# A mixture-of-experts layer that starts on full tiles: the last block's output and routing as steps between the experts' products

## The chip, the cores and the metric

The kernel runs on one core of a Trainium2 chip. The metric is the device time of one execution in microseconds (us). The engines of a core are TensorE (PE; its weight loads are listed as PEld), VectorE (DVE), ScalarE (ACT), GpSimd (POOL) and SyncE (SP), which here only starts transfers and reads the registers that they need. A transfer is started ("issued") by an engine's queue and carried out by the core's 16 DMA engines.

## The reference

A picture of 64 x 64 points with 256 channels goes through four layers. Only the last two matter here. Written out for N = 4096 tokens t of C = 256 channels:

```python
# layer 3, attention: one head, all tokens
n = layernorm(t); q, k, v = n @ Wq + bq, n @ Wk + bk, n @ Wv + bv
t = t + softmax(q @ k.T / 16) @ v
# layer 3, mixture of 8 experts, the two best for each token
n = layernorm(t); probs = softmax(n @ Wg + bg); w, e = top_k(probs, 2); w = w / w.sum()
t = t + sum(w[r] * (gelu(n @ W1[e[r]] + b1[e[r]]) @ W2[e[r]] + b2[e[r]]) for r in (0, 1))
```

W1 is 256 x 1024 and W2 is 1024 x 256 for each expert. Layer 2 ends in a mixture of the same form with a hidden size of 256 and its own weights. Everything is float32.

## The kernel before

**Blocks and tiles.** The 4096 tokens are 8 blocks of 512 (`NBLK`, `NB`), each of 4 groups of 128 (`TPB`). Every token is listed at two experts, so 8192 rows stand in a list in DRAM (`xs`), one stretch of 4096 rows for each expert. The expert work goes in tiles of 256 rows of one expert (`MT`). An expert's last tile may be partly filled, so up to 39 tiles may be needed (`NTILE`); 36 of them (`MOST`) are always worked out, and the last three stand under a condition that the counts decide.

**Attention (`attn3`, L2385).** For each block of queries, 16 steps (`g`, with 16 pairs of key groups) run on PE: `scores(g)`, and two steps later (`LAG`) `values(g - 2)`. Both are products in a form with seven instead of eight block products, so DVE adds and subtracts parts before and after them (L2534 to L2537, L2552, L2570 to L2572), and ACT takes the exponentials (L2566). After the last step of a block its output stands in `oT`. `finish` (L2595) multiplies it by the value weights for one group of 128, divides, and adds to the tokens `t`. In the steps of the next block, indices j = 0 to 3 finish the four groups of the previous block, j = 4 starts its `route`, and j = 6, 8, 10, 12, 14 each run one of the routing's five stages:

1. statistics, square root (ACT), norm, all on DVE but the root
2. transposing one half of the channels on PE (`turn`, L2061), copied by ACT
3. transposing the other half, copied by DVE
4. the router's logits (16 small matmuls), the two best experts (`top2`, DVE), the exponential (ACT), weights, and the running count per expert (`cum`)
5. positions of the rows in the lists (a small product on PE, `place`), `find` on DVE, and 8 scatters of 128 rows each to `xs` by POOL (L2113)

In this part the order on PE and POOL is the one written (`tc.manual_schedule`), and the other engines are ordered by a planner. The last block, number 7, has no next block to be hidden under: its four `finish` and all five routing stages follow after attention's last matmul (L2662 to L2666), and then `tile_table` (L2121), about 40 small DVE instructions. The table says for each tile which expert it belongs to (`tab[:, 0]`), where its rows begin (`tab[:, 1]`), and how many are valid.

**Experts (`experts`, L2173; `expert_tiles`, L2190).** For each tile, SP reads expert and row from the table into registers and loads the tile's rows (260 KB) and the expert's weights w1 and w2 (1028 and 1152 KB; L2204, L2209, L2211), two tiles ahead. `turn` transposes the rows on PE, `first` makes the hidden rows with 32 matmuls and Gelu on ACT, `sides` makes four sums of weights on POOL (`f_wt`, L2259), `where` finds the target rows and weights on DVE, and `second` multiplies by w2, again with seven products, and scatters the result to DRAM (`ys`, L2302). The loop runs `first` of tile i, `turn` of tile i + 1, then `second` of tile i - 1. The planner orders all engines. The same code serves layer 2, with sizes of its own.

**Memory.** SBUF and PSUM are given out in pools that open and close with the stages. Attention's pools (`a3`, `a3w`, `a3_ps`) hold the values, the working tiles and the routing's `room` (the normed rows that the scatters read). They close before the expert pools (`f3e`, `f3e_ps`) open. PSUM has 8 banks; in the expert stage the transposed rows have two, the hidden rows three, the two parts of the output three.

Of the kernel before, what the change touches and what calls it, by code (L numbers as in the profile page):

```python
# [29 lines left out]
NE = 8  # L30
# [19 lines left out]
NI = MT // P  # L50

# [37 lines left out]
class Net:  # L89
# [2031 lines left out]
    def tile_table(self, S, wp, bank):  # L2121


        nc = self.nc
        tl = lambda shape, tag, dt=F32: wp.tile([P] + shape, dt, tag="f_" + tag, name="f_" + tag, bufs=1)
        c_ps = bank()[:, :NE]
        self.mm(c_ps, [(self.all_one, S["cum"])])

        ci = tl([NE], "ci", I32)
        nc.vector.tensor_copy(ci, c_ps)  # L2130
        nc.vector.tensor_single_scalar(ci, ci, MT - 1, ALU.add)
        nc.vector.tensor_single_scalar(ci, ci, MT.bit_length() - 1, ALU.arith_shift_right)
        cnt = tl([NE], "cnt")
        nc.vector.tensor_copy(cnt, ci)
        ends = tl([NE], "ends")
        nc.vector.tensor_tensor_scan(ends, self.one.to_broadcast([P, NE]), cnt, 0.0, ALU.mult, ALU.add)

        last = tl([1], "last")
        nc.vector.tensor_scalar_add(last, ends[:, NE - 1 : NE], -1.0)
        tau = tl([NTILE], "tau")  # L2140
        nc.vector.tensor_scalar(tau, self.count, last, None, ALU.min)
        past = tl([NTILE, NE], "past")
        nc.vector.tensor_tensor(past, bc(ends, 1, NTILE), bc(tau, 2, NE), ALU.is_le)
        ex = S["ex"]
        nc.vector.tensor_reduce(ex, past, AX.X, ALU.add)
        tab = S["tab"]
        nc.vector.tensor_scalar_mul(tab[:, 0, :], ex, float(P))
        nc.vector.tensor_tensor(past, past, bc(cnt, 1, NTILE), ALU.mult)
        skip = tl([NTILE], "skip")
        nc.vector.tensor_reduce(skip, past, AX.X, ALU.add)  # L2150
        nc.vector.tensor_sub(tau, tau, skip)
        nc.vector.tensor_scalar_mul(tau, tau, float(MT))
        nc.vector.scalar_tensor_tensor(skip, ex, float(N), tau, ALU.mult, ALU.add)
        nc.vector.tensor_copy(tab[:, 1, :], skip)
        rows = tl([NE], "rows")
        nc.vector.tensor_copy(rows, c_ps)
        nc.vector.tensor_copy(S["used"], ends[:, NE - 1 : NE])

        nc.vector.tensor_tensor(past, bc(ex, 2, NE), bc(self.count[:, :NE], 1, NTILE), ALU.is_equal)
        nc.vector.tensor_tensor(past, past, bc(rows, 1, NTILE), ALU.mult)  # L2160
        nc.vector.tensor_reduce(skip, past, AX.X, ALU.add)
        nc.vector.tensor_sub(skip, skip, tau)
        nc.vector.tensor_scalar(tau, self.count, last, None, ALU.is_le)
        nc.vector.tensor_mul(skip, skip, tau)

        nc.vector.tensor_tensor(S["in"], bc(self.nth[:, :NI], 1, NTILE), bc(skip, 2, NI), ALU.is_lt)
        nc.vector.tensor_scalar(S["off"], S["in"], -1.0, 1.0, ALU.mult, ALU.add)
        for i in range(0, NTILE, 4):
            n = min(4, NTILE - i)
            part = S["off"][:, i : i + n, :].rearrange("p i k -> p (i k)")  # L2170
            nc.vector.scalar_tensor_tensor(part, self.nth[:, : n * NI], float(2 * N), part, ALU.add, ALU.mult)

    def experts(self, S):  # L2173

        tc = self.tc

        def some(tiles):
            with (
                tc.tile_pool(name=f"f{S['L']}e", bufs=5 if S["L"] == 2 else 3) as wp,
                tc.tile_pool(name=f"f{S['L']}e_ps", bufs=1, space=PSUM) as ps,  # L2180
            ):
                self.expert_tiles(S, tiles, wp, ps)

        some(range(MOST))
        used = self.nc.values_load(S["used"][0:1, 0:1], min_val=0, max_val=NTILE,
                                   skip_runtime_bounds_check_because="worked out from counts of tokens")
        with tc.If(used > MOST):
            some(range(MOST, NTILE))

    def expert_tiles(self, S, tiles, wp, ps):  # L2190
        nc, A = self.nc, self.A
        L, tab = S["L"], S["tab"]
# [5 lines left out]
        def load(i):  # L2198
            e = nc.values_load(tab[0:1, 0, i : i + 1], engines=[mybir.EngineType.SP], min_val=0, max_val=(NE - 1) * P,
                               skip_runtime_bounds_check_because=why)  # L2200
            row = nc.values_load(tab[0:1, 1, i : i + 1], engines=[mybir.EngineType.SP], min_val=0, max_val=NE * N - MT,
                                 skip_runtime_bounds_check_because=why)
            x = wp.tile([P, NI, CX], F32, tag="x", name="f_x", bufs=ahead + 3)
            rows = lambda: nc.sync.dma_start(out=x, in_=self.xs[bass.ds(row, MT), :].rearrange("(i p) c -> p i c", p=P))  # L2204

            if i > 0:
                rows()
            w1 = wp.tile([P, 2 * hidden + KH], F32, tag="w1", name="f_w1")
            nc.sync.dma_start(out=w1, in_=A[f"f{L}_w1"][bass.ds(e, P), :])  # L2209
            w2 = wp.tile([P, KH * C + C], F32, tag="w2", name="f_w2")  # L2210
            nc.sync.dma_start(out=w2, in_=A[f"f{L}_w2"][bass.ds(e, P), :])  # L2211
            if i == 0:
                rows()
            return x, w1, w2

        def turn(x):
            p = ps.tile([P, 2, MT], F32, tag="x", name="f_x_ps", bufs=2)
# [17 lines left out]
        def where(i, x):  # L2235
# [3 lines left out]
            op = nc.vector  # L2239
            op.tensor_scalar(first, x[:, :, C + 3], S["ex"][:, i : i + 1], None, ALU.is_equal)  # L2240
# [4 lines left out]
            op.tensor_tensor(to, to, S["in"][:, i, :], ALU.mult)  # L2245
            op.tensor_tensor(at, to, S["off"][:, i, :], ALU.add)
# [60 lines left out]
        tiles = list(tiles)  # L2307

        nc.scalar.activation(wp.tile([P, 1], F32, tag="g", name="f_gelu", bufs=1), self.one, AF.Gelu)
        ld = {i: load(i) for i in tiles[:ahead]}  # L2310
        xT = turn(ld[tiles[0]][0])
        to = where(tiles[0], ld[tiles[0]][0])
        done = None
        for i in tiles:
# [4 lines left out]
            now = (i, h, w2, sides(w2)) + to  # L2319
            if i < tiles[-1]:  # L2320
                xT = turn(ld[i + 1][0])
                to = where(i + 1, ld[i + 1][0])
            if done is not None:
                second(*done)
            done = now
        second(*done)

    def outputs(self, b, y):

        src = self.ys[: 2 * N, :].rearrange("(r b p i) c -> b p r (i c)", r=2, b=NBLK, i=TPB)  # L2330
        for r in range(2):
            (self.nc.sync, self.nc.scalar)[r].dma_start(out=y[:, r].rearrange("p i c -> p (i c)"), in_=src[b][:, r])
# [10 lines left out]
    def moe_state(self, pool, L=2):  # L2343
        tl = lambda shape, tag, dt=F32: pool.tile([P] + shape, dt, tag=tag, name="f_" + tag)
        return {
            "L": L, "to": tl([2, NT], "to", I32), "tab": tl([2, NTILE], "tab", I32), "used": tl([1], "used", I32),
            "big": tl([2, 2, NT // 2], "big"), "r": tl([NT], "r"), "ex": tl([NTILE], "ex"), "in": tl([NTILE, NI], "in"), "off": tl([NTILE, NI], "off"),
# [37 lines left out]
    def attn3(self, t, S):  # L2385
# [6 lines left out]
        with (  # L2392
            tc.tile_pool(name="a3", bufs=1) as pool,
            tc.tile_pool(name="a3d", bufs=1, space=DRAM) as dpool,
        ):

# [8 lines left out]
            wvp = pool.tile([P, 2, C + 1], F32, tag="wvp", name="a3_wvp")  # L2405
# [12 lines left out]
            with (  # L2418
                tc.tile_pool(name="a3w", bufs=2) as wp,
                tc.tile_pool(name="a3_ps", bufs=1, space=PSUM) as ps,  # L2420
            ):
# [4 lines left out]
                def bank(few=False):  # L2426
                    banks.append(banks.pop(0))
                    return ps.tile([P, NB], F32, tag=banks[-1], name="a3_q_ps")

                room = lambda: wp.tile([P, TPB * CX + 2 * NB], F32, tag="room", name="f_room")  # L2430
# [3 lines left out]
                def add(b):  # L2434

                    y = room()[:, : 2 * TPB * C].rearrange("p (r i c) -> p r i c", r=2, c=C)
                    self.outputs(b, y)
                    part = t[:, b * TPB : (b + 1) * TPB, :]
                    for r in range(2):
                        nc.vector.tensor_tensor(part, part, y[:, r], ALU.add)  # L2440
# [33 lines left out]
                def ask(b, m):  # L2474

                    ks = kss[b]
                    if m == 0:
                        nc.vector.memset(vs[:, 2 * b : 2 * b + 2, 1 : 4 : 2, P - 1 : P], 1.0)

                        qTs[b] = wp.tile([P, 2, NB], F32, **(dict(tag="oT", name="a3_qT", bufs=1) if b else dict(tag="q", name="a3_q")))  # L2480
# [14 lines left out]
                def route(t0, T):  # L2495
                    r = room()
                    n = r[:, : TPB * CX].rearrange("p (i c) -> p i c", c=CX)
                    rT = r[:, TPB * CX :].rearrange("p (k n) -> p k n", k=2)
                    return self.route(t0, T, t, S, wp, n, rT, bank)
# [75 lines left out]
                def values(g):  # L2575
# [11 lines left out]
                    if j == NPAIR - 1:  # L2587
                        oT = oTs[b] = wp.tile([P, 2, 2, QB], F32, tag="oT", name="a3_oT", bufs=1)
# [55 lines left out]
                with tc.manual_schedule(engines={ET.PE, ET.Pool}):  # L2644
                    steps = iter(())
                    for g in range(first, G + LAG):
# [6 lines left out]
                        if b > 0:  # L2653
# [4 lines left out]
                            elif j % 2 == 0:  # L2658
                                next(steps, None)
                    for _ in steps:  # L2660
                        pass
                    banks += ["sa", "sb", "sc"]  # L2662
                    for i in range(TPB):
                        finish(NBLK - 1, i)
                    for _ in route((NBLK - 1) * TPB, TPB):
                        pass  # L2666
                with tc.manual_schedule(engines={ET.PE, ET.Pool, ET.DVE}):
                    self.tile_table(S, wp, bank)
# [88 lines left out]
    def run(self, x, out):  # L2757
        tc, nc = self.tc, self.nc
        with tc.tile_pool(name="const", bufs=1) as cpool, ExitStack() as left:
# [20 lines left out]
            with tc.tile_pool(name="tok", bufs=1) as tpool:  # L2780
# [5 lines left out]
                with tc.tile_pool(name="moe", bufs=1, side="right") as mpool:  # L2786
# [9 lines left out]
                    self.experts(S)  # L2796
# [127 lines left out]
```

## Time and profile before

| What | us |
|---|---|
| median of 10 runs | 3423.87 |
| fastest and slowest of them | 3421.54, 3433.22 |
| the profiled execution's own time | 3433.52 |
| its span, first to last instruction | 3431.8 |
| PE busy in the span | 3105.9 (91%) |
| DVE busy | 2303.8 (67%) |
| ACT busy | 1328.7 (39%) |
| POOL busy | 1455.5 (42%) |

The profile's page gives busy time by engine, then the span in 40 equal slices of 85.8 us, a digit for the busy tenths in each, then the granted TensorE clock (PEclk) in the same slices. A timeline row holds the start in us from the span's start, its length, engine and line, the operation with what it writes and reads, the shape, and how many instructions are put together; in brackets stands how long the engine had been idle before and what ended it. A q behind the engine's name marks an instruction of its queue. Layer 3's attention runs from about 1930 to 2835 us, its experts to about 3381 us.

### The profile page before, as it was taken

Reading aid. Unit: us, or ns where it says so; the run is one execution under the profiler, and the core shown is the slowest. Engines: PE = TensorE matmul, PEld = TensorE weight load, DVE = VectorE, ACT = ScalarE, POOL = GpSimd, SP = SyncE. Lnnn points to the kernel's source line nnn. Section 1 sums busy time; section 2 is a strip of 40 time slices with the busy share of each in tenths; the row PEclk is TensorE's granted clock in tenths of the full one; section 3 lists DMA queues with packets and bytes.
Section 4 is the critical chain, followed back from the end, with each engine's and each line's share of the span. In section 5 each row is a group of like instructions: output and inputs, shape, how many; then the busy total and the mean of one; then the engine's idle time right before and its main releaser. Section 6 shows DMA issues by size and latency. Waiting matters only on the chain.

```text
span 3431.8 us, 66162 instructions
## 1 busy us (share of the span) xinstructions
PE 3105.9 (91%) x25772; PEld 2324.7 (68%) x25772; DVE 2303.8 (67%) x5315; ACT 1328.7 (39%) x2550; POOL 1455.5 (42%) x1316
## 2 busy tenths in 40 slices
PE   6779999999977899897969789999999996999997
PEld 3443444344436888666847567888888885999996
DVE  8885777577754677796855576777777775555552
ACT  4444344444425666243633352222222222333331
POOL 2028788878834555343544352000000003555552
PEclk9889999999988999897979899999999997999998
DMA  1145555521133222100158643322333314555554
GB/s 71 43 113 145 160 154 169 133 65 52 49 122 106 68 75 74 42 1 2 64 198 266 208 182 107 104 87 93 99 99 99 98 56 160 194 196 208 205 199 175
DMA packets 241688, 407.01 MB, mean 119 GB/s; under 512 B 78353, under 2 KB 152850, under 8 KB 231890
## 3 DMA queue, kind: packets, MB, share of 16 engines
q1 hardware_dynamic: 212002, 344.40, 31.7%
q0 software_dynamic: 13056, 35.93, 2.8%
q10 hardware_dynamic: 16304, 22.31, 2.0%
q8 instruction: 207, 3.39, 0.4%
q14 instruction: 119, 0.97, 0.1%
HBM read 287.07 MB, written 111.30 MB: 116 GB/s over the span
## 4 chain that ended last, share of the span: by engine, by line
PE 42%; DVE 9%; DMA 6%; issue 5%; ACT 3%; POOL 3%; SPq 0%; POOLq 0%; DVEq 0%; ACTq 0%
PE a_sa_ps L2547 6%; PE f_h_ps L148 5%; DMA ys<-f_y,f_at 3%; PE l_acc_ps L1156 3%; PE a_oa_ps L2586 3%; PE a_ob_ps L2586 3%; PE a_oc_ps L2586 3%; PE a_sb_ps L2547 3%; PE f_ya_ps L148 2%; PE f_yb_ps L148 2%; DVE l_pr L1152 2%; PE a_od_ps L2586 1%; POOL ys L2302 1%; PE a_q_ps L148 1%; PE a_sc_ps L2547 1%
## 5 line engine op out<-in xcount | busy, mean ns | idle before, releaser
L772 ACT COPY l_sc<-l_s 128x384 f32<-128x384 f32 (+1 forms) x632 | 304.0, 532 | 451.2 <-PE l_s L765 440.6
L777 DVE TENSOR_TENSOR l_sm<-l_s,mask 128x256 f32<-128x256 f32 (+2 forms) x628 | 307.9, 550 | 90.5 <-PE l_s L765 89.4
L148 PE MATMUL f_h_ps<-f_xT,f_w 128*128 128x256 f32 x1440 | 340.7, 388 | 21.8 <-DVE f_xT L2222 13.1
L2113 POOL DMA_INDIRECT xs<-f_room,f_to x64 | 64.3, 1004 | 697.3 <-issue 582.6
L148 PEld LDWEIGHTS f_h_ps<-f_xT,f_w 128*128 128x128 f32 x1440 | 262.2, 192 | 85.5 <-ACT f_h L2232 29.6
L765 PE MATMUL l_s<-l_q,l_k 32*128 32x256 f32 (+3 forms) x2944 | 270.4, 453 | 0.0
L2566 ACT ACTIVATE a_e<-a_e 128x512 f32<-128x512 f32 x256 | 155.9, 629 | 246.0 <-DVE a_e L2536 242.9
L782 POOL TENSOR_TENSOR l_sm<-l_sc,mask 128x768 f32<-128x768 f32 (+1 forms) x116 | 202.4, 1752 | 87.8 <-ACT l_sc L772 87.7
L2232 ACT ACTIVATE f_h<-f_h_ps,f_w 128x256 f32<-128x256 f32 x360 | 166.6, 470 | 187.9 <-PE f_h_ps L148 187.9
L1152 DVE TENSOR_TENSOR l_pr<-l_vk,l_w_ps 128x1280 f32<-128x1280 f32 x128 | 186.7, 1481 | 55.2 <-PE l_acc_ps L1156 37.6
L765 PEld LDWEIGHTS l_s<-l_q,l_k 32*128 32x128 f32 x2944 | 132.3, 183 | 115.2 <-issue 67.5
L2302 POOL DMA_INDIRECT ys<-f_y,f_at x144 | 146.5, 1018 | 142.8 <-ACT f_y L2301 112.7
L1156 PE MATMUL l_acc_ps<-ident,l_pr 128*128 128x128 f32 x1600 | 198.2, 278 | 7.7 <-POOL l_pr L1147 7.6
L1156 PEld LDWEIGHTS l_acc_ps<-ident,l_pr 128*128 128x128 f32 x1600 | 184.8, 144 | 14.2 <-POOL l_pr L1147 8.6
L786 POOL TENSOR_TENSOR l_sm<-l_sc,mask 128x256 f32<-128x256 f32 (+1 forms) x220 | 184.9, 868 | 15.4 <-ACT l_sc L772 14.5
L2259 POOL TENSOR_TENSOR f_wt<-f_w 128x512 f32<-128x512 f32 x72 | 89.9, 1270 | 216.6 <-PE f_ya_ps L148 205.0
L2547 PE MATMUL a_sa_ps<-a_q,a_kt 128*128 128x256 f32 x512 | 155.3, 385 | 13.6 <-DVE a_u L2552 12.8
L2551 ACT COPY a_u<-a_sa_ps 128x256 f32<-128x256 f32 x128 | 47.6, 372 | 293.0 <-PE a_sa_ps L2547 293.0
L811 PE MATMUL l_b_ps<-l_sm,l_v 128*32 128x256 f32 (+2 forms) x2176 | 153.4, 372 | 0.0
L2547 PE MATMUL a_sa_ps<-a_qt,a_kt 128*128 128x256 f32 x512 | 152.4, 379 | 0.0
L782 POOL TENSOR_TENSOR l_sm<-l_sc,mask_c 128x768 f32<-128x768 f32 (+1 forms) x64 | 120.1, 1894 | 37.0 <-ACT l_sc L772 36.5
L2547 PE MATMUL a_sb_ps<-a_qt,a_kt 128*128 128x256 f32 x512 | 132.3, 381 | 0.0
(558 smaller groups left out, 7290.1 us busy)
## 6 DMA issues: line engine op xcount, KB each, us to landing
a_kt<-a_kd SPq DMA_DIRECT2D x128, 512.0 KB
f_w<-in_f_w SPq DMA_DIRECT2D x36, 1152.0 KB
f_w<-in_f_w SPq DMA_DIRECT2D x36, 1028.0 KB
xs<-zero SPq DMA_DIRECT2D x8, 4160.0 KB
l_vk<-vt SPq DMA_DIRECT2D x180, 128.0 KB
f_x<-xs SPq DMA_DIRECT2D x72, 260.0 KB
f_w<-in_f_w SPq DMA_DIRECT2D x36, 384.0 KB
l_rcp<-l_recd SPq DMA_DIRECT2D x48, 256.0 KB
```

Source lines behind the costliest of these rows:

```text
L148: self.nc.tensor.matmul(out, lhsT, rhs, start=(i == 0), stop=(i == len(pairs) - 1))
L765: nc.tensor.matmul(s[pair, j][:, at : at + m, :], key(hp), qs[hp], start=(z == 0), stop=(z == len(pieces) - 1))
L772: nc.scalar.copy(sc[:, j], s[1, j])
L777: nc.vector.tensor_tensor(to(pair, j, kind, at), pick(s[pair, j], kind, which), mask, ALU.mult)
L782: nc.gpsimd.tensor_tensor(out[:, :, at, :], of[:, :, which, :], bc(mask, 1, 2), ALU.mult)
L786: nc.gpsimd.tensor_tensor(to(1, j, kind, at), pick(sc[:, j], kind, which), mask, ALU.mult)
L1152: nc.vector.tensor_tensor(pr, vk, bc(held["w"][:, j, dy], 3, D), ALU.mult)
L1156: nc.tensor.matmul(acc[:, m, j, :], pf[:, dx, m * P : (m + 1) * P], self.ident, is_transpose=True, start=(j == 0 and dy == 0 and dx == 0 a ...
L2232: nc.scalar.activation(h[:, m, :], q, AF.Gelu, bias=w1[:, 2 * hidden + m : 2 * hidden + m + 1])
L2302: nc.gpsimd.indirect_dma_start(out=self.ys_parts[(i % 4) * NI + k], in_=y[:, k, :], in_offset=None, out_offset=bass.IndirectOffsetOnAxis(a ...
L2547: mm = lambda out, i, right: nc.tensor.matmul(out, A[i], right, start=True, stop=True)
L2586: nc.tensor.matmul(out, vs[:, j, i, :], right, start=(j == 0 and side != 1), stop=(j == NPAIR - 1 and side != 0))
```

## The change

- A new table, `full_table`, is made from the counts of blocks 0 to 6 alone. 7168 of the 8192 rows are known by then, and at most 255 of each expert's rows don't fill a tile, so at least 20 tiles (`FULL`) are full whatever block 7 adds. They are table "A". `gone` notes how many tiles of each expert it holds. `tile_table`, when called early, makes table "B" of the 19 others, from the counts of all blocks less `gone`; for layer 2 it makes all 39 as before.
- Block 6's routing stages run at j = 5 to 9, one at each step of the loop, and `full_table` at j = 10.
- Attention's pools close directly after the loop. What block 7 still needs stands in two pools opened before them, `k3` and `k3_ps`: the value weights, the output `oT`, the routing's `room` (one instead of two) and small tiles, and one PSUM bank.
- `experts` gets seven steps, run one at a time: the four `finish` before the first tile's rows are turned, then the first routing stage, then one stage after `first` of tile 0, after `first` of tile 1, after `second` of tile 0, and after `first` of tile 2; after `second` of tile 1 table B is made. Block 7's rows are thus scattered to `xs` when the rows of tiles 0 to 4 have been asked for, and before those of tile 5.
- PE's order in the third layer's experts is the one written, and the transposed rows have one PSUM bank there instead of two.
- `add`, which fetches layer 2's results at attention's start, takes three rooms for half a fetch each instead of two for a whole one.

The diff, cut to its core:

```diff
+FULL = (2 * (N - NB) - NE * (MT - 1)) // MT
+    def full_table(self, S, wp, bank):
+        T, n = S["A"], FULL
+        c_ps = bank()[:, :NE]
+        self.mm(c_ps, [(self.all_one, S["cum"])])
+        nc.vector.tensor_copy(ci, c_ps)
+        nc.vector.tensor_single_scalar(ci, ci, MT.bit_length() - 1, ALU.arith_shift_right)
+        nc.vector.tensor_copy(full, ci)
+        nc.vector.tensor_tensor_scan(ends, self.one.to_broadcast([P, NE]), full, 0.0, ALU.mult, ALU.add)
+        nc.vector.tensor_tensor(past, bc(ends, 1, n), bc(self.count[:, :n], 2, NE), ALU.is_le)
+        nc.vector.tensor_reduce(T["ex"], past, AX.X, ALU.add)
+        nc.vector.tensor_scalar_mul(T["tab"][:, 0, :], T["ex"], float(P))
+        nc.vector.tensor_tensor(past, past, bc(full, 1, n), ALU.mult)
+        nc.vector.tensor_reduce(tau, past, AX.X, ALU.add)
+        nc.vector.tensor_sub(tau, self.count[:, :n], tau)
+        nc.vector.tensor_scalar_mul(tau, tau, float(MT))
+        nc.vector.scalar_tensor_tensor(tau, T["ex"], float(N), tau, ALU.mult, ALU.add)
+        nc.vector.tensor_copy(T["tab"][:, 1, :], tau)
+        nc.vector.tensor_sub(gone, full, ends)
+        nc.vector.tensor_scalar(gone, gone, float(n), 0.0, ALU.add, ALU.max)
+        nc.vector.tensor_tensor(gone, gone, full, ALU.min)
+        nc.gpsimd.memset(T["in"], 1.0)
+        nc.gpsimd.memset(T["off"], 0.0)
...
+        if early:
+            nc.vector.tensor_sub(cnt, cnt, S["gone"])
...
-        some(range(MOST))
+        tiles = [("A", i) for i in range(FULL)] if early else []
+        rest = [("B", i) for i in range(NTILE - len(tiles))]
+        tiles += rest[:-3]
...
+                if early:
+                    order.enter_context(tc.manual_schedule(engines={mybir.EngineType.PE}))
+                self.expert_tiles(S, tiles, wp, ps, list(steps), 1 if early else 2)
...
-            p = ps.tile([P, 2, MT], F32, tag="x", name="f_x_ps", bufs=2)
+            p = ps.tile([P, 2, MT], F32, tag="x", name="f_x_ps", bufs=x_banks)
...
         ld = {i: load(i) for i in tiles[:ahead]}
+        step()
         xT = turn(ld[tiles[0]][0])
         to = where(tiles[0], ld[tiles[0]][0])
+        step()
         done = None
         for i in tiles:
...
             now = (i, h, w2, sides(w2)) + to
+            step()
             if i < tiles[-1]:
...
                 second(*done)
+                step()
...
-                    y = room()[:, : 2 * TPB * C].rearrange("p (r i c) -> p r i c", r=2, c=C)
-                    self.outputs(b, y)
+                    ys = [wp.tile([P, TPB, C], F32, tag="room", name="f_room", bufs=3) for r in range(2)]
+                    self.outputs(b, ys)
...
-                            elif j % 2 == 0:
+                            elif j % 2 == 0 or b == NBLK - 1:
                                 next(steps, None)
-                    for _ in steps:
-                        pass
-                    banks += ["sa", "sb", "sc"]
-                    for i in range(TPB):
-                        finish(NBLK - 1, i)
-                    for _ in route((NBLK - 1) * TPB, TPB):
-                        pass
-                with tc.manual_schedule(engines={ET.PE, ET.Pool, ET.DVE}):
-                    self.tile_table(S, wp, bank)
+                            if b == NBLK - 1 and j == TPB + 6:
+                                self.full_table(S, keep, bank)
+            left.close()
+            last = route((NBLK - 1) * TPB, TPB)
+            def finished():
+                for i in range(TPB):
+                    finish(NBLK - 1, i)
+            go = lambda: next(last, None)
+            self.experts(S, [finished, go, go, go, go, go, lambda: self.tile_table(S, keep, bank, True)])
```

## The prediction

> **What bounds the kernel now.** I read the page first, for its row of PE by slice, then the busy times in windows round the change, then the timeline and the chain of waits between 2834 and 2882 us. PE is 91% busy over the span, and the stages on both sides of the change are full of it:
>
> ```profile
> PE   6779999999977899897969789999999996999997
> ...
> PEclk9889999999988999897979899999999997999998
> ```
>
> The one hole beside the change is slice 34 (the 6 of PE, from 2831 us). The windows show it in busy us of PE, PEld, DVE, ACT and POOL, then the granted clock, the DMA share and GB/s:
>
> ```profile
> 2769.00:2793.00 24.00, 24.00 (x112) 21.01 (x112) 17.23 (x38) 7.11 (x13) 0.00 (x0) 1.00 0.29 89
> 2835.00:2840.00 5.00, 3.87 (x17) 2.74 (x15) 4.10 (x15) 0.00 (x0) 3.84 (x4) 1.00 0.31 108
> 2850.00:2855.00 5.00, 1.54 (x6) 1.43 (x6) 3.87 (x28) 1.49 (x2) 0.00 (x0) 0.50 0.00 0
> 2855.00:2860.00 5.00, 0.00 (x0) 0.00 (x0) 4.58 (x17) 0.00 (x0) 3.82 (x4) 0.50 0.23 80
> 2870.00:2875.00 5.00, 0.00 (x0) 0.00 (x0) 0.00 (x0) 0.00 (x0) 0.00 (x0) 0.50 0.99 403
> 2885.00:2890.00 5.00, 5.00 (x23) 4.23 (x22) 2.58 (x11) 2.37 (x5) 1.96 (x2) 0.92 0.57 228
> 3100.00:3200.00 100.00, 99.03 (x661) 90.19 (x660) 54.62 (x142) 35.93 (x83) 55.76 (x45) 1.00 0.55 199
> ```
>
> Attention (first row) and the products (last row) keep PE full with the other engines at 72% or less. Between them PE stands still for over 20 us, and its granted clock falls to 0.50 until 2885. The timeline names what fills the hole:
>
> ```profile
> 2834.54 0.59 PE L2586 MATMUL a_oc_ps<-a_et,a_vs 128*128 128x256 f32 x2
> 2835.37 0.68 DVE L2537 TENSOR_TENSOR a_oT<-a_u,a_oc_ps 128x512 f32<-128x512 f32 x1
> ...
> 2864.41 0.96 POOL L2113 DMA_INDIRECT xs<-f_room,f_to  x1 [0.30 <-issue]
> 2867.22 0.34 SPq L2209 DMA_DIRECT2D f_w<-in_f_w  x1
> 2867.54 1.28 ACT L2309 ACT_TABLE_LOAD   x1 [14.87 <-DMA xs<-f_room,f_to]
> ...
> 2875.99 1.94 PE L2220 MATMUL f_x_ps<-ident,f_x 128*128 128x128 f32 x8 [22.39 <-DMA f_x<-xs]
> ```
>
> Attention's last matmul ends at 2835.13. The last block's output, routing, 8 scatters and the table follow, then the first weight load at 2867.22, the first rows on PE at 2875.99, the first product (L2232's operand, line 148) at 2881.71: **46.6 us**, with a few us of PE work in them. The ACT row tells what the loads wait for: this table load belongs to an activation on a constant (L2309), yet it waits for the last scatter's landing. So the expert tiles' memory is given as a whole when the attention pools, routing room among them, are done.
>
> **The change part by part.** All times below are in the profiled execution (span 3431.8, own time 3433.52 us, 9.65 above the median of 3423.87); I carry the difference over to the median.
>
> *The first loads.* They now need only the table of full tiles, made five steps earlier, and the end of the attention pools: the last reader of those is L2537, done at 2836.05. A wait of 0.38 us from release to issue (scatter landed 2866.84, issue 2867.22) gives 2836.4 instead of 2867.22: **-30.8**. From this load to the first product I keep the 14.5 us of before (2867.22 to 2881.71), 8.7 of them until the rows land.
>
> *The output products (4 x finish).* They now share one bank: product to product 1.7 us by an earlier block's row (matmul from 2764.7, L2602 done 2766.27), 6.8 in all, under the 8.7 us until the rows land: nothing. If the clock halves in them, 4 x 0.9 more, and rows wait 2 us. Norm and statistics (DVE, about 4 us) lie under the same wait.
>
> *Attention's end.* Block 6's routing has steps 6 us apart instead of 12 (one step of the loop took 6.04 us). PE work is the same; only the distance shrinks. From logits to running count the chain took 3.7 us on a free DVE (2849.03 to 2852.7); the loop's own DVE work is 4.15 of 6.04 us (0.42+0.41+0.69+0.42+0.68+0.69+0.42+0.42), so 1.9 are free and the position product, next on PE's fixed order, waits 1.8. Queued behind it are the scores, for which DVE and ACT wait. The new table costs 0.3 us of PE and about 3.3 of DVE (11 operations at 0.15 to 0.19; four on 160 elements, a shape not in the trace, between 0.22 for 64 and 0.48 for 312, taken as 0.32). Seven steps with 1.9 free each cover it; where it stands in front of L2552, PE loses some, 1.0. Together **+3.1**, between 0.3 and 8.1 (nothing of 3.7+0.8+3.3 covered, and 0.3).
>
> *Routing between products.* Formerly in the hole, now in PE's time: two turns at 0.44, logits 1.79, positions 0.45, table 0.3: **+3.4**. Before each stands a product of 6.9 us (32 matmuls) or 6.3, so that norm and copies are ready. The exception is the position product, after first(2), with the next turn and second(1) queued behind it: DVE has 7.4 us of work per tile of 13.6 (54.62 per 100), and 3.7 of top-2 come in half a tile. The second table's roughly 7 us of DVE fall in the next tile, which has 6.2 free. I take **+2.0** for these waits, between 0 and 8 (3.7 + 7, less the 3 free in half a tile).
>
> *Queues.* SP: rows of tiles 0 to 4 are read ahead of the last block's scatters, which wait for them; the rows of tile 5 wait for the scatters, with its weights behind them. From the first product to the positions are 32 us (three firsts, one second, turns, logits, 2 at half clock). find 1.3, POOL 8 x (0.96+0.30) = 10.1, landing 2.43 and 6.7 for the rows: there at 53. They are needed at 60: 7 us spare, nothing. POOL works 7.6 us a tile; ten more delay wt, which has a tile's time. The new table's two memsets meet an idle POOL (0.00 in the first row of the windows).
>
> *At nothing:* the single bank for transposed rows (its copy is done 13 us before it is wanted); PE's order by hand (the trace has just this order: f_h, f_x, f_ya/f_yb); 36 tiles as before. Three half rooms instead of two whole ones in add: the fourth read waits for the first add (done 1938.55), lands by about 1942.5 by the 3.6 us of the first one, and is added after 1943.67; without this cover 2 us. The clock: in both kernels PE idles before the first product; it came back 4.1 us after it, and I keep that. Without the drop, 2 us less.
>
> *Sqrt and Exp among Gelus* raise ACT's table loads from 3 to 5. The row says 1.28 us, with the activation 0.02 later (2766.89, then 2768.19). ACT idles 5.3 us in each second half, so nothing in the sum. The Trainium skill ("ScalarE: Activation LUTs", "Rules for kernel authors") speaks against this: group activations by table set, each switch costs about 2.7 us with its drain. By the page two more switches put 5.3 us on ACT, an estimate of its figure, which would just fill that idle time and leave the sum as it is. The row shows no drain.
>
> Sum: -30.8 + 3.1 + 3.4 + 2.0 = -22.3. Profiled 3411; median 3423.9 - 22.3 = **3402**.
>
> **The rivals.**
> *Loads earlier still.* If memory is given tile by tile, loads run under attention, and the first product waits for the output products: 6.8 plus turn and copy 1.3 after 2839.2, so 2847.3 instead of 2854.0: 3395. The ACT row speaks against it.
> *DVE is the bound at both seams.* Attention's end 8.1 and waits 8: -30.8+8.1+3.4+8 = -11.3, 3413. For it: 72% busy in attention, and in-order waits; against: those steps had no stall over 0.7 us when 12 us apart.
> *It doesn't take effect.* If the expert memory still waited for the last block's rows, their steps would stand behind the product that needs it; that can't run. What remains is a gain eaten almost whole, within 7 us: 3420.
> *Slower: the scatters come late on POOL.* Tile 5's rows, and SP's queue behind them, stand until they land. If POOL takes wt and the outputs of later tiles first (7.6 us each), the 7 us spare are gone after one tile; the change loses from 7 + 22 = 29 us late, four tiles. At six tiles it is 3440. Against: the scatters are ready first.
>
> **How the numbers follow.** Forecast 0.59, earlier loads 0.10, DVE 0.16, nothing left 0.06, late scatters 0.09. Range 3388 to 3418: from the best ends together (loads 6.7 earlier, waits 2.0 and attention's end 2.8 less, no clock drop 2: 3402 - 13.5) to the DVE case (3413) with 2 us each for the output products and for the rooms, and 1 of ACT's loads. It holds the forecast, the earlier loads and most of the DVE case. Faster by over 0.2% (6.8 us; about what can be told from no change) 0.85, within 0.06, slower 0.09.
>
> **What would show it.** First load at or before 2840 and first product near 2854; gelu's early table load waiting for attention, not scatters; the loop step before block 6's position product near 8 us; between products PE idle of some 2 us, with a row of tile 5 landing before its turn. A first load after 2850, PE waits over 10 us among tiles 0 to 6, or a tile period above 13.6 us would prove me wrong.

## The result, and the profile after

| | before | after |
|---|---|---|
| median, us | 3424.03 (28 runs, 3418.25 to 3433.22) | 3527.86 (8 runs, 3520.70 to 3534.44) |
| ratio, 95% interval | | 1.0301 [1.0291, 1.0312] |
| profiled execution: own time / span, us | 3433.52 / 3431.8 | 3534.23 / 3532.5 |

The change costs 103.8 us where a gain of 22 was forecast. In the page's rows by slices the single 6 beside the change has become two 7s, but the 9s behind it have turned to 8:

```profile
PE   6779999999977999879697899999999977888886
...
PEclk9889999999988999989798999999999989999999
```

A slice is 88 us: 33 and 34, from 2826 us, hold the seam, and 35 to 39 the experts' steady run. The windows of the kernel after, with the columns as before (busy us of PE, PEld, DVE, ACT, POOL, then clock, DMA share, GB/s):

```profile
2827.00:2882.00 55.00, 38.50 (x180) 28.79 (x179) 31.94 (x88) 14.15 (x26) 15.38 (x12) 0.83 0.42 161
2882.00:2955.00 73.00, 57.25 (x308) 45.84 (x308) 37.42 (x134) 20.35 (x42) 31.64 (x29) 0.89 0.45 158
3100.00:3200.00 100.00, 86.16 (x538) 72.53 (x537) 41.51 (x119) 28.93 (x66) 45.10 (x36) 1.00 0.46 167
```

The last row is the one to look at. Far from the seam, where the change was thought to alter nothing, PE does 538 matmuls in 100 us, where before it did 661, at the same full clock; every other engine is less busy too, and DMA as well. So none of them is the bound; PE waits for something. The first rows say that the early loads did come. Timeline of the seam, after:

```profile
2826.56 0.60 PE L2649 MATMUL a_oc_ps<-a_et,a_vs 128*128 128x256 f32 x2
...
2827.39 0.68 DVE L2600 TENSOR_TENSOR a_oT<-a_u,a_oc_ps 128x512 f32<-128x512 f32 x1
...
2828.14 1.28 ACT L2365 ACT_TABLE_LOAD   x1 [2.68 <-DVE a_oT L2600]
...
2828.27 0.34 SPq L2265 DMA_DIRECT2D f_w<-in_f_w  x1
...
2836.90 1.09 PE L2276 MATMUL f_x_ps<-ident,f_x 128*128 128x128 f32 x4 [2.13 <-DMA f_x<-xs]
...
2843.10 2.08 PE L152 MATMUL f_h_ps<-f_xT,f_w 128*128 128x256 f32 x4 [5.12 <-DVE f_xT L2278]
```

The table load, which waited for the last scatter, now waits for attention's `a_oT` alone; the first weight load stands right behind it, and the first product comes 15.95 us after attention's last matmul (2827.15) instead of 46.6. What the steady tiles wait for is in the list of waits from the first product to the end (us in total, times, longest), first after:

```profile
PEld f_h_ps L152 <- ACT f_h L2288: 146.5, 143, 4.3
...
PE f_h_ps L152 <- ACT f_h L2288: 87.3, 143, 3.9
```

and before:

```profile
PEld f_h_ps L148 <- ACT f_h L2232: 13.0, 42, 0.9
...
PE f_h_ps L148 <- ACT f_h L2232: 4.4, 9, 0.5
```

The products of hidden rows wait for the gelu, four times a tile (143 is 4 x 36, less one). One tile on PE, after:

```profile
3102.92 1.03 PE L152 MATMUL f_h_ps<-f_xT,f_w 128*128 128x256 f32 x4
3104.56 2.00 PE L152 MATMUL f_h_ps<-f_xT,f_w 128*128 128x256 f32 x8 [0.61 <-ACT f_h L2288]
3107.12 1.99 PE L152 MATMUL f_h_ps<-f_xT,f_w 128*128 128x256 f32 x8 [0.56 <-ACT f_h L2288]
3109.68 2.00 PE L152 MATMUL f_h_ps<-f_xT,f_w 128*128 128x256 f32 x8 [0.56 <-ACT f_h L2288]
3112.24 1.13 PE L152 MATMUL f_h_ps<-f_xT,f_w 128*128 128x256 f32 x4 [0.56 <-ACT f_h L2288]
3113.21 0.60 PE L2276 MATMUL f_x_ps<-ident,f_x 128*128 128x128 f32 x4
```

Each 128 hidden rows are 4 matmuls here. The groups are 4, 8, 8, 8, 4: a wait stands before the 2nd, 4th, 6th and 8th set of 128, that is before each second half of a PSUM bank. `first` writes two halves into one tile `p` of [P, 2, MT] floats, 2 KB of a partition, and the gelu of the first half stands between the two products in the text. From the first of these matmuls to the transpose it is 10.29 us; the same 32 without a wait take 6.91 (below). The tile's period, from one tile's transposes to the next one's, is 16.98 us far from the seam. Before, it was 13.62, with 14.37 every third or fourth time.

Three stretches of the traces carry the rest of this text: **A**, the second experts, first product to last output product; **B**, from the second matmul of attention's last group of value products (3.0 us before the last one's end) to the first product of the third experts; **C**, the third experts, first product to last output product.

| us | ratio to before (95%) | A | B | C |
|---|---|---|---|---|
| before | | 168.4 | 49.5 | 498.3 |
| after | 1.0301 [1.0291, 1.0312] | 166.0 | 18.9 | 639.7 |
| e1, both products, then gelus | 0.9952 [0.9931, 0.9972] | 164.3 | 19.0 | 513.8 |
| e2, planner orders PE | 0.9949 [0.9930, 0.9969] | 164.1 | 19.5 | 511.9 |
| e3, before, PE by hand | 1.0351 [1.0331, 1.0371] | 165.0 | 49.6 | 617.5 |
| e4, before, one bank for rows | 1.0000 [0.9990, 1.0011] | 166.9 | 49.2 | 499.6 |
| e5, e1 with more places | 0.9887 [0.9866, 0.9908] | 150.7 | 18.9 | 505.9 |
| e6, e1, table in pieces | 0.9952 [0.9937, 0.9968] | 162.3 | 18.9 | 510.8 |
| e7, e1, rows first | 0.9935 [0.9914, 0.9957] | 166.2 | 12.8 | 510.1 |
| e8, e5 + e6 + e7 | 0.9861 [0.9839, 0.9884] | 148.5 | 12.1 | 505.3 |
| e9, e5, steps ahead of products | 0.9915 [0.9888, 0.9943] | 149.3 | 33.6 | 497.0 |
| e10, before, more places | 0.9939 [0.9920, 0.9958] | 151.7 | 49.0 | 491.7 |
| e11, half a bank each | 0.9963 [0.9948, 0.9979] | 166.1 | 19.1 | 514.0 |
| e12, e8 with DVE by hand | 0.9828 [0.9814, 0.9841] | 150.0 | 12.3 | 498.4 |

Each ratio is to runs of the kernel before that were made together with its own; the medians below come from several such groups, which differ by a few us. In the nine kernels whose small tables have four buffers (all but e5, e8, e9, e10 and e12) A lies between 162.3 and 168.4, and the second experts' first product starts between 1748.7 and 1759.0 us in these profiles: a few us up to attention's end are the execution's own. So B and C are compared, not spans. After against before: B -30.6, C +141.4, attention's end reached 8.0 earlier, what follows C 2.1 shorter; together the 100.7 by which the spans differ.

### The profile page after: what moved, and what is told of

Its sections match the earlier page's. It is cut to its first block, busy times and chain, and to the rows that moved or that the text cites. A ratio compares the mean times of both kernels' runs of the same rounds, so it can differ in the third digit from the quotient of the medians.

```text
span 3532.5 us, 66250 instructions
## 1 busy us (share of the span) xinstructions
PE 3141.3 (89%) x25774; PEld 2317.4 (66%) x25774; DVE 2296.2 (65%) x5331; ACT 1332.6 (38%) x2552; POOL 1457.0 (41%) x1318
## 5 line engine op out<-in xcount | busy, mean ns | idle before, releaser
L152 PE MATMUL f_h_ps<-f_xT,f_w 128*128 128x256 f32 x1440 | 387.4, 406 | 112.3 <-ACT f_h L2288 92.3
L1160 PEld LDWEIGHTS l_acc_ps<-ident,l_pr 128*128 128x128 f32 x1600 | 184.9, 144 | 12.8 <-POOL l_pr L1151 7.6
L790 POOL TENSOR_TENSOR l_sm<-l_sc,mask 128x256 f32<-128x256 f32 (+1 forms) x220 | 184.9, 868 | 14.2 <-ACT l_sc L776 13.3
L2649 PE MATMUL a_ob_ps<-a_et,a_vs 128*128 128x256 f32 x512 | 131.5, 379 | 0.0
```

The lines of the kernel that those rows point to most:

```text
L152: self.nc.tensor.matmul(out, lhsT, rhs, start=(i == 0), stop=(i == len(pairs) - 1))
L790: nc.gpsimd.tensor_tensor(to(1, j, kind, at), pick(sc[:, j], kind, which), mask, ALU.mult)
L1160: nc.tensor.matmul(acc[:, m, j, :], pf[:, dx, m * P : (m + 1) * P], self.ident, is_transpose=True, start=(j == 0 and dy == 0 and dx == 0 a ...
```

## The experiments

The theory **T1**: in the order written by hand, the second product into a PSUM bank waits for the gelu of the first. The rivals: **T2**, the single bank for transposed rows; **T3**, the last block's steps and scatters between the products. Four kernels tell them apart.

**e1**, the changed kernel with the text of `first` turned round:

```diff
-                nc.scalar.activation(h[:, m, :], q, AF.Gelu, bias=w1[:, 2 * hidden + m : 2 * hidden + m + 1])
+                if m % 2:
+                    for k in (m - 1, m):
+                        nc.scalar.activation(h[:, k, :], p[:, k % 2, :], AF.Gelu, bias=w1[:, 2 * hidden + k : 2 * hidden + k + 1])
```

> The changed kernel with one edit: both products of a PSUM bank of hidden rows are written before the two gelus that read it; PE's order stays by hand. T1 (by hand, the second product into a bank waits for the gelu of the first: four waits of about 0.6 us on PE and 1.0 on the weight load in each of 36 tiles, some 3.2 us a tile): the tile's period falls from 16.98 to about 13.7, the kernel to 3528 - 115, about 3413. Rival T2 (one bank in place of two for the transposed rows) and rival T3 (the last block's routing and its scatters between the products): nothing changes, 3528 within 5.

Measured: 3410.96 us. The 32 matmuls run through, and the transpose follows 6.91 us after their start; timeline of e1:

```profile
3004.73 7.07 PE L152 MATMUL f_h_ps<-f_xT,f_w 128*128 128x256 f32 x32
3011.64 0.60 PE L2276 MATMUL f_x_ps<-ident,f_x 128*128 128x128 f32 x4
```

The period is 13.60, 3.38 less, as the tile above would have it (10.29 - 6.91). Moving one line of text on ACT is worth some 117 us. T2 and T3 are both in this kernel and cost nothing like it.

**e2**, the changed kernel, planner in place of hand:

```diff
-                if early:
-                    order.enter_context(tc.manual_schedule(engines={mybir.EngineType.PE}))
```

> The changed kernel without the hand-written order of PE in the third experts: the planner orders them, as in the kernel before; one bank for transposed rows and the routing steps stay. T1: the banks of hidden rows alternate again, period about 13.7, the kernel about 3405 to 3415. T2: period stays 17.0, 3528. T3: 3528 within 10, as the steps still run between the products.

Measured: 3410.95, tiles of 13.62 and 14.37 far from the seam, as before. In its order of instructions, as in that of the kernel before, a tile's hidden rows alternate between two banks, A B A B and then two others: the planner had put the gelu of one bank under the products of the other. That is not in the text of either kernel. The traces, which leave out the buffers' numbers, fit it: where the weight load of a set of four matmuls is held up there, it starts behind the gelu of the set two places earlier (before: a load at 3103.02, that gelu's end at 3102.96), in e3 below behind that of the set just before (3103.29 and 3103.24).

**e3**, the kernel before, with only this added:

```diff
+                if S["L"] == 3:
+                    order.enter_context(tc.manual_schedule(engines={mybir.EngineType.PE}))
```

> The kernel before with PE's order by hand in the third experts alone: two banks for transposed rows, no early table, no steps. T1: period 17.0 for 13.8, so 36 x 3.2 = 115 more, about 3538. T2 and T3: 3424 within 5, since neither of their causes is there.

Measured: 3547.83, C 617.5 against 498.3: **119.2 us from the hand-written order alone**. Its waits are those of the changed kernel, without any of its steps:

```profile
PEld f_h_ps L148 <- ACT f_h L2235: 141.7, 144, 1.3
PE f_h_ps L148 <- ACT f_h L2235: 82.9, 144, 0.6
```

**e4**, the kernel before with `bufs=2 if L == 2 else 1` for `f_x_ps`.

> The kernel before with one bank in place of two for the transposed rows of the third experts, all else as it was. T1 and T3: 3424 within 5, because a tile's rows are copied out of the bank some 10 us before the next tile writes it. T2: about 3 us a tile, 3530.

Measured: 3426.08, ratio 1.0000. T2 falls; the step "the single bank for transposed rows" at nothing was right.

**e11** asks whether it is the bank, or merely that product and gelu take turns in the text. The changed kernel's order is left as it is, each 128 rows get a bank of which half stays unused (in the second experts too):

```diff
-                if m % 2 == 0:
-                    p = ps.tile([P, 2, MT], F32, tag="h", name="f_h_ps", bufs=3)
-                q = p[:, m % 2, :]
+                p = ps.tile([P, 2, MT], F32, tag="h", name="f_h_ps", bufs=3)
+                q = p[:, 0, :]
```

> The changed kernel, its written order untouched (product, gelu, product, gelu), with each 128 hidden rows in a PSUM bank of their own: three banks of which only half is used. T1 (the wait is for the gelu of the other half of the same bank): period 13.6 to 13.8, 3410 within 8. Rival T12 (what costs is that product and gelu take turns in the written order, whatever bank they use, or that three banks are too few when each is reused after three products): period stays above 15, over 3460.

Measured: 3414.82, periods far from the seam 13.60, with 14.37 every third or fourth. The sets run through; timeline of e11:

```profile
3007.17 7.07 PE L152 MATMUL f_h_ps<-f_xT,f_w 128*128 128x256 f32 x32
3014.08 0.60 PE L2276 MATMUL f_x_ps<-ident,f_x 128*128 128x128 f32 x4
```

With the same text, the four waits in every tile are gone once the two halves lie in different banks (10 waits in all, for 143). It is the shared bank. Here a bank and the tile `p` are one and the same, and no run parts them: whether the wait goes by the one or the other isn't shown. The Trainium skill says why a wait must stand there ("PSUM — Partial Sum Buffer", "PSUM bank collisions raise a hardware error": two engines may not touch the same 32 partitions of one bank at once, even at different addresses, so semaphores guard the bank) and what to do ("Perfetto Trace Analysis", "Matmuls": let independent products rotate through banks). e1, e3 and e11 agree with both, with 3.4 us a tile as the price here.

**What the repaired change is worth, and what stands in its seam.** e1 has B 30.5 less and C 15.5 more than before. Three places in its trace look dear. First, the ACT and PE rows of e1 round one late tile, with DVE and POOL beside them:

```profile
2892.98 3.90 DVE L2196 TENSOR_TENSOR f_tau<-f_tau,f_skip 128x19 f32<-128x19 f32 x1
...
2900.03 4.40 DVE L2298 TENSOR_SCALAR f_first<-f_x,f_exA 128x2 f32<-128x2 f32 x1
```

```profile
2893.12 2.50 POOL L2317 TENSOR_TENSOR f_wt<-f_w 128x512 f32<-128x512 f32 x2
2895.57 2.67 POOL L2317 TENSOR_TENSOR f_wt<-f_w,f_wt 128x512 f32<-128x512 f32 x2
...
2900.68 2.48 POOL L2317 TENSOR_TENSOR f_wt<-f_w 128x512 f32<-128x512 f32 x2
2903.12 3.11 POOL L2317 TENSOR_TENSOR f_wt<-f_w,f_wt 128x512 f32<-128x512 f32 x2
```

```profile
2910.91 0.91 ACT L2359 ACTIVATE f_y<-f_y,f_wgt 128x256 f32<-128x256 f32 x2 [8.14 <-DVE f_y L2352]
...
2912.23 3.78 PE L152 MATMUL f_h_ps<-f_xT,f_w 128*128 128x256 f32 x8 [6.56 <-ACT f_h L2290]
```

Read from the end: PE waits 6.56 us for a gelu; the gelu stands on ACT behind the weighting of the tile before; that waits 8.14 us for `f_y`; and DVE, 98% busy from 2890 to 2910, has the second table's instructions among the tile's own. Two of all these last about 4 us while POOL runs `f_wt`, 8.3 of the 20 us. This tile takes 22.17 us. Second, the first product waits 5.12 us for DVE's copy `f_xT`, behind the norm. Third, six later tiles take 14.84 to 15.26. One edit for each:

**e5** gives the small tables of `where` eight buffers, `bufs=8` for 4 (in the second experts too).

> e1 with eight buffers in place of four for the small tables of rows (f_first to f_at). T4 (DVE stands in order behind f_at, which waits until the scatter of four tiles earlier has read its buffer; f_y, ACT's weighting and the next gelu come late by that): the six tiles of 14.84 to 15.26 us fall to 13.60, some 7 us less than e1, about 3404. Rival T5 (those tiles are late for some other reason, such as POOL holding DVE up): unchanged against e1, 3411 within 3.

Measured: 3385.53. From the seventh on all periods are 13.60, as T4 had it, which makes up the 7.9 us by which C falls. The rest came where I had not looked: A falls by 13.7, for the second experts run the same `where`. **e10** makes the same edit in the kernel before:

> The kernel before with eight buffers in place of four for the small tables of rows, in the second and the third experts alike, nothing else. If f_at's wait is what e5 removed: the second experts take about 151 us for 168 (e5's 150.6 against 164.3 in e1) and the third experts' tiles of 14.37 fall to 13.62, some 7; together 20 to 24 less than before, about 3400. If the gain of e5 needed the hand-written order: 3424 less 15 at most.

Measured: 3405.95, A 151.7, C 491.7: 16.7 and 6.6 less, and no tile of 14.37 is left. Before, DVE's wait stood in the list of waits within A (1760 to 1925 us); in e10's list DVE's `f_at` no longer waits for it:

```profile
DVE f_at L2246 <- DMA ys<-f_y,f_at: 60.1, 31, 5.7
```

So this is not the change's gain, but an old cost of both kernels: `f_at` may be overwritten only when the scatter four tiles earlier has read it.

**e6** writes the second table in seven pieces and the scatters in four pairs, each a step:

```diff
+            *([(("place",), ("find",))] + [(("scatter", [i]),) for i in range(T)] if spread else [(("place",), ("find",), ("scatter", range(T)))]),
...
-            self.experts(S, [finished, go, go, go, go, go, lambda: self.tile_table(S, keep, bank, True)])
+            table = self.tile_table(S, keep, bank, True)
+            self.experts(S, [finished] + [go] * 9 + [lambda: next(table, None)] * 7)
```

> e1 with the second table written in seven pieces and the last block's eight scatters in four pairs, each piece and pair a step of its own between the products. T6 (the 40 small DVE instructions of the second table stand among tile 3's and tile 4's own, DVE is 98% busy for 20 us, f_y is late and the gelus behind it): the tile of 22.17 falls to about 14, some 8 us less than e1, about 3403. Rival T7 (the time goes to the long waits of small DVE instructions while POOL runs f_wt, wherever they stand): the loss moves to other tiles, 3408 to 3411.

Measured: 3404.54, but C is only 3.0 less than e1's, and the ratio is the same. The tile of 22.17 falls to 14.95; tiles of 16.86, 14.67, 15.34 and 18.43 come up elsewhere. Nearer to T7 than to T6. But DVE isn't ordered by hand, and the planner has put the seven pieces back into one run, in e6 from 2907 to 2918 us and in e8 from 2890 to 2909: pieces in the text were no pieces on the engine, so e6 tested little of either theory.

**e7** loads the first rows ahead of the first weights and turns them before the last `finish`:

```diff
-            if i > 0:
+            if i > 0 or L == 3:
                 rows()
...
-                for i in range(TPB):
+                for i in range(TPB - 1):
                     finish(NBLK - 1, i)
+            def begun():
+                finish(NBLK - 1, TPB - 1)
+                next(last, None)
```

> e1 with the first tile's rows loaded ahead of its weights, and turned before the last of the four tiles of attention's output is finished. T8 (the first product waits for DVE's copy of the turned rows, 5.1 us behind the norm and small table work, after 2.2 us for the rows' transfer): first product 5 to 7 us earlier, about 3405. Rival T9 (the first weights' landing sets it): the rows go ahead of the weights, which land some 0.7 us later; 3410 to 3412.

Measured: 3399.72; B falls by 6.2 us to 12.8, T8. **e8** puts the three together:

> e5, e6 and e7 together. T4, T6 and T8: the sum of theirs, some 20 us less than e1, about 3391. If their rivals hold: 3405 to 3411.

Measured: 3375.32. More was won than the sum, since A's 16 were in no theory; of the 20 that were foreseen for B and C, 15.4 came, and one tile still takes 19.60.

**e9** asks what running the steps between the products is worth: e5 with all of them ahead of the first product.

> e5 with all steps of the last block (output, routing, second table) run in one piece ahead of the first product; the first loads stay early. T10 (running the steps between the products hides most of their time): the first product comes 20 to 25 us later than in e5 and the tiles' seams win back under 8, about 3400. Rival T11 (between the products the steps cost about what they hide: e5's first six tiles take 14 us more than six of 13.60): first product 15 to 20 later, 12 to 14 won back, 3386 to 3393.

Measured: 3394.76; B + C is 530.6 against e5's 524.8. The steps ahead cost 14.7 us of B and win back 8.9 of C: hiding them is worth 5.8 us in these two profiles; the intervals of the two ratios overlap. That lies between the two theories, nearer to T11, whose sizes were both somewhat too large. The gain is in the early loads; the steps between the products, as e5 places them, are nearly a draw.

**e12** is e8 with DVE by hand as well, the hidden rows' sums moved up:

```diff
-                    order.enter_context(tc.manual_schedule(engines={mybir.EngineType.PE}))
+                    order.enter_context(tc.manual_schedule(engines={mybir.EngineType.PE, mybir.EngineType.DVE}))
...
-            done = now
+            done = now + (halves(h),)
```

> e8 with DVE's order by hand too in the third experts, and a tile's four sums of hidden rows written behind the output of the tile before, so that PE finds them ready. T13 (in e8 the planner put the seven pieces of the second table back together between 2889 and 2908 us, and one tile took 19.60; by hand each piece stays where it is written): that tile falls to about 14, some 7 us less than e8, about 3368. Rival T14 (in a fixed order DVE stands behind waits for transfers and for the exponential, so that other tiles come late): 3375 or more.

Measured: 3371.00, ratio 0.9828: **the fastest**, where the change as it was had 1.0301. C is 6.9 less than e8's; behind the fourth period none is over 13.82, and the pieces of the table stand apart on DVE, from 2902 to 2942 us. That is T13. The sums, moved in the same run, weren't tried alone. The long DVE instructions beside `f_wt` are still there (this one takes at most 1.69 us in e1), without a late tile; timeline of e12:

```profile
2897.28 4.41 DVE L2366 TENSOR_TENSOR f_y<-f_y,f_w 128x512 f32<-128x512 f32 x1
```

Against e10, the kernel before with the same larger tables, B is 36.7 less and C 6.7 more: 30.0 for the repaired change, with the edits of e6, e7 and e12.

## Why the prediction was wrong, by its own steps

**The step that failed:** "*At nothing:* [...] PE's order by hand (the trace has just this order: f_h, f_x, f_ya/f_yb)". True between groups, false inside `f_h`. The rows of the trace join equal forms, with the buffer numbers left out; the order of banks inside them was the planner's and nowhere in the text. The rows of before did hold a hint: 24 matmuls in one go, with a gelu due after every fourth in the text. Timeline of before:

```profile
3099.68 5.36 PE L148 MATMUL f_h_ps<-f_xT,f_w 128*128 128x256 f32 x24
3104.88 0.60 PE L2220 MATMUL f_x_ps<-ident,f_x 128*128 128x128 f32 x4
```

Asking "what waits for what, if the text is the order" would have found one bank with two halves and a gelu between them. Its cost is 119.2 us (e3), shown by adding it alone, and taking it away alone (e1, e2, e11). No rival in the prediction held it; the slower one, late scatters, was another mechanism. The prediction's sign of being wrong, "a tile period above 13.6 us", came true as 16.98, though the kernel before has periods of 14.37 too.

**The first loads, -30.8: right.** B fell by 30.6; the load's distance from `a_oT` (0.2 us after its end at 2828.07) and the table load's releaser are as forecast.

**Attention's end, +3.1: too much.** The last block's steps, among which block 6's routing now stands at half the distance, take 94.6 us from the first value product to the last, for 94.4 before: 0.2 us. Each value holds to 0.03 us in every kernel with its order (e3, e4 and e10; e1, e2, e5 to e9, e11 and e12).

**The output products through one bank, nothing: right.** They took 7.4 us from `a_oT`'s end to the last addition (6.8 forecast) and were done, at 2835.49, before the rows were turned at 2836.90. From first load to first product 14.83 us were measured for the 14.5 kept; that this stretch held a wait of 5.12 us for DVE, which e7 could take away, wasn't seen.

**Routing between products, +3.4 and +2.0: too small.** With the order repaired and the tables' old cost removed on both sides, C is 14.2 us longer than before's (e5 505.9, e10 491.7), for a forecast of 5.4. The waits come to 14.2 - 3.4 = 10.8, over even the bound of 8. I had put the second table's 7 us of DVE into "6.2 free"; its place was one tile in which two small DVE instructions lasted 4 us beside POOL's `f_wt`. In the kernel as changed there is also this, which the prediction called "7 us spare, nothing" on POOL, and which is a wait on DVE:

```profile
2923.20 1.03 DVE L2302 TENSOR_TENSOR f_at<-f_to,f_offA 128x2 int32<-128x2 f32 x1 [5.81 <-DMA ys<-f_y,f_at]
...
2925.49 2.07 PE L152 MATMUL f_h_ps<-f_xT,f_w 128*128 128x256 f32 x4 [5.51 <-DVE f_xT L2278]
```

The eight scatters to `xs` (POOL, 2898.23 to 2908.33), and one tile's `f_wt` behind them, stood in front of the scatters of outputs, which start at 2913.56; `f_at` waited for those, and PE for the copy queued behind it. I had asked who waits for the rows of tile 5, not who waits for POOL's next scatters.

**Sqrt and Exp among the gelus, nothing: right with the order repaired.** In the kernel as changed, the two table loads round the exponential (2883.29 and 2884.81, 1.28 us each) stand before a gelu for which PE waits 2.32 us; in e1 no such wait is left.

Taken together, with e10 and e5 as the two kernels without either defect, the change is worth -30.1 + 14.2 = -15.9 where -22.3 was forecast, and -11.3 by the rival "DVE is the bound at both seams", whose price for the waits between the products was the nearer one and whose price for attention's end was not. So the mechanism of the gain was right; one edit costed at nothing, because it seemed to repeat what was there, was five times larger than all that.

## What to carry to other kernels

Before an engine's order is taken from the planner, write out the order that it had made, instruction by instruction with the buffers' numbers, and compare it with the text: a loop "product, activation, product, activation" over halves of one PSUM bank is serial the moment the text is obeyed, so write both products first or give each a bank. When work is moved between an engine's instructions, price it against the fixed-order engines that hold it up, and where only one engine is ordered by hand, look where the planner has put the pieces on the others: in e6 and e8 it had joined them again. And look at what the tuned kernel already waits for: four buffers in place of eight for tables of 1 KB cost both kernels over 20 us (A and C together).

## What of the hardware was not expected

Small DVE instructions last very differently beside POOL. `f_first`, 128x2, takes 0.23 us in e1 (median); one took 4.40 us, and a 128x19 one 3.90, both ending within POOL's run of `f_wt`. The Trainium skill ("SBUF — State Buffer", "SBUF: two separate sides") says that a DVE instruction with two inputs in SBUF, or in a two-port mode, and one of GpSimd hold a shared pair of ports in turn, for a whole instruction, whichever starts first. The rows agree in part: both end within 0.05 us behind the third of POOL's four instructions (2896.84 and 2904.39), but by the profile both had started before its first (by 0.14 and 0.65 us). No run here separates this from other causes. The granted clock fell again after single PE waits of 5 to 7 us: 0.66 in e1 between 2910 and 2920, behind the wait of 6.56, and 0.50 in the changed kernel between 2925.4 and 2930, behind the one of 5.51. The four waits of about 0.56 us in every tile left it at 1.00 far from the seam, as the row of windows shows; but in the changed kernel's first tiles it fell as well (0.57 between 2860 and 2864, 0.72 between 2880 and 2886, 0.57 between 2890 and 2895), where no single wait was longer than 2.32 us. So these rows give no length of wait at which it falls.
